# Conv products of all batches: the imaginary part accumulated in the first product's PSUM bank, copied out by ScalarE

## The chip, the cores and the metric

The kernel runs on one core of one Trainium2 chip. The metric is the device time of one execution in microseconds (us), taken as the median of several runs. Engines are named as in the profile: PE is TensorE (PEld its weight loads), DVE is VectorE, ACT is ScalarE, POOL is GpSimd, SP is SyncE, which issues nearly all DMAs. In the profile one fp32 matmul of the program is two passes on PE, so the profile counts 10004 PE instructions.

## The reference, cut to what matters

Two graph layers over 64 graphs of 256 nodes with 256 features, all in fp32. In the first layer:

```
h      = relu(bn1(conv1 @ x^T))                       # 1x1 convolution
x_conv = relu(bn2(conv2(h), 17 taps, along the nodes) + x)
A      = exp(-dist(x @ w_se)) * adj;  x_nmp = A @ relu(x @ w_msg)
gi     = [x_conv, x_nmp] @ w_ih^T;  gh = x @ w_hh^T   # GRU gates r, z, n
x      = layernorm(x + (1 - z) * n + z * x)
```

The second layer is a layernorm, an aggregation with `adj`, two 256x256 projections, a relu, a residual and a layernorm. The change concerns only the 17-tap convolution `conv2`.

## The kernel before, in words

**The convolution.** The graphs are handled in eight batches of eight. Each batch's sequences of 256 nodes are cut into overlapping pieces of 32, and the 17-tap convolution is done as a product of polynomials: DVE splits the data step by step into 15 complex residues and 2 real ones (`split`, `butterflies`), PE multiplies each residue by the filter's residue (a 256x256 matrix), and DVE merges them back (`merge`). A complex product takes three real ones: k1 is the filter's c times (re + im), k2 is (d - c) times re, k3 is (c + d) times im; the new real part is k1 - k3, the new imaginary part k1 + k2. The data lie in the SBUF tile `XF`, seen as slots `X` of 128 x 256; the sums re + im are in slots of their own. Each real product of one slot is four matmuls (two halves of the output features, two of the input features), of 128 moving columns each: eight passes on PE (L718).

**The groups.** Complex residues are multiplied in pairs, so that a group fills 512 columns of a PSUM bank. A batch has seven such groups (`products`, L721) and a last one of different shape (`last_products`, L759). For every batch but the first, the filter's residues come from DRAM: `load_w` (L706) loads three matrices (768 KB) for one residue into one of `W_DEEP` = 2 buffers in the tile `cs`. In the first batch (b = 0) all filters still lie in SBUF, in `w2all`.

**Two ways to end a group.** For b > 0, `products` uses three banks: p1, p2, p3. When all six products of the pair are done, ACT copies p1 to the slots of the sums (L735), DVE writes the real part as copy - p3 (L736) and the imaginary part as copy + p2 (L737). For b = 0, `products_added` (L740) uses two banks: the first product of both residues goes to p1, ACT copies p1 out (L748), the third goes to p3, and then the second product is accumulated onto p1, which now holds the imaginary part. ACT copies that to the data's slots (L755), and DVE does the one subtraction (L756).

**The rest of the work.** Beside the convolution, 32 pairs of graphs go through `pair`: messages (L1088), distances (L1125), aggregation (L1139), gates (L1191, a seven-product scheme for 2x2 block matrices; plain in L1177 for three pairs), normalisation, projection (L1366), second aggregation (L1380). The convolution of batch b + 1 is spread over the time in which the four pairs of batch b are worked on.

**What sets the order.** Nothing is issued in program order. All operations are recorded (`Program`, `Engine`), each with a key, which is a due time, and an estimated duration. `scheduled` (L320) then writes out one fixed order per engine: of the operations that could start, the one with the smallest key goes first; PSUM banks are handed out in the same pass, with at most three for the share "conv". PE operations that have been ready for 0.7 us are preferred (`READY`). The constants in L58 to L66 set the keys: `FIRST_GATES` and `PERIOD` when pairs are due, `CONV_FROM`, `CONV_OUT`, `CONV_TO` where a batch's convolution is spread, `LOAD_AHEAD` how much earlier than its place a load is keyed, `KEEP` the spacing of the copies of the finished convolution. On the chip each engine works through its list in order and waits where an input or a buffer is not there.

Of the kernel before, what the change touches and what calls it, by code (L numbers as in the profile page):

```python
# [32 lines left out]
NB = B // BG  # L33
# [21 lines left out]
OB = 7  # L55
HQ = 2 * M * C * (M + 1)
XC_SLOTS = BG + 2
FIRST_GATES, PERIOD, GATE_TIME = 115.5, 58.7, 14.1  # L58
AHEAD_FROM, AHEAD_TO, W_DEEP = -49.7, -53.1, 2
CONV1_FROM, CONV1_TO, CONV_FROM, CONV_OUT, CONV_TO = -29.4, 99.1, -10.5, -47.1, -26.3  # L60
PAIR_LEAD, FILTER_LEAD, LOAD_AHEAD = 50.5, 7.3, 20.3
SMALL_RUNS, TURN_FROM = 1.3, 2
KEEP = 13.3
LATE_LAG = 28.9
W_FROM, W_LAG = 2, 42.0
COORDS = 41.8  # L66
PLAIN, SUMS_FROM = (0, 1, B // 2 - 1), 2


# [349 lines left out]
def gnn_two_layers(  # L419
# [32 lines left out]
    def bank(name, share="rest"):  # L452
        return Space(name, [P, 512], "psum", share, share if share in ("conv", "gate") else None).view
# [127 lines left out]
    def sl(a, n, step=1):  # L581
        return X[:, a:a + n] if step == 1 else X[:, a:a + (n - 1) * step + 1:step]
# [123 lines left out]
    def load_w(b, first, n):  # L706
        if b == 0:
            return lambda m, c: W2[:, c, first + m, :]
        at = next(w2_at) * 3 * C * D
        t = cs[:, at:at + 3 * C * D].rearrange("p (m c o) -> p m c o", m=3, c=C)  # L710
        SP.dma_start(out=t[:, :n], in_=w2m[first:first + n].rearrange("f c p o -> p f c o"))
        return lambda m, c: t[:, m, c, :]

    def product(ps, slot, w, m, first=True):
        with prog.group():
            for o in range(C):
                for c in range(C):
                    PE.matmul(ps[:, o * P:(o + 1) * P], w(m, c)[:, o * P:(o + 1) * P], X[:, slot, c * P:(c + 1) * P],  # L718
                              start=first and o == 0 and c == 0, stop=(c == C - 1), skip_group_check=True)

    def products(b, first, sums):  # L721
        if b == 0:
            return products_added(first, sums)
        p1, p2, p3 = (bank(f"ps_k{i}", "conv") for i in (1, 2, 3))
        re, im, _ = LEAVES[first]
        for k in range(2):
            w = load_w(b, 3 * (first + k), 3)
            at = slice(k * D, (k + 1) * D)
            product(p1[:, at], sums + k, w, 0)
            product(p2[:, at], re + k, w, 1)  # L730
            product(p3[:, at], im + k, w, 2)

        def take():
            k1 = sl(sums, 2).rearrange("p s e -> p (s e)")
            A.copy(k1, p1)  # L735
            V.tensor_sub(sl(re, 2).rearrange("p s e -> p (s e)"), k1, p3)  # L736
            V.tensor_add(sl(im, 2).rearrange("p s e -> p (s e)"), k1, p2)  # L737
        return take

    def products_added(first, sums):  # L740
        p1, p3 = (bank(f"ps_k{i}", "conv") for i in (1, 3))
        re, im, _ = LEAVES[first]
        w = [load_w(0, 3 * (first + k), 3) for k in range(2)]
        at = [slice(k * D, (k + 1) * D) for k in range(2)]
        k1 = sl(sums, 2).rearrange("p s e -> p (s e)")
        for k in range(2):
            product(p1[:, at[k]], sums + k, w[k], 0, k == 0)
        A.copy(k1, p1)  # L748
        for k in range(2):
            product(p3[:, at[k]], im + k, w[k], 2)  # L750
        for k in range(2):
            product(p1[:, at[k]], re + k, w[k], 1, False)

        def take():
            A.copy(sl(im, 2).rearrange("p s e -> p (s e)"), p1)  # L755
            V.tensor_sub(sl(re, 2).rearrange("p s e -> p (s e)"), k1, p3)  # L756
        return take
# [102 lines left out]
    def conv(b):  # L860
# [8 lines left out]
        if b == 0:  # L869
            run(other)  # L870
        sv, s8, s4 = {}, {}, {}
        todo = [(lambda k=k: products(b, 2 * k, S + 2 * k), merges(0, k, S, sv, True)) for k in range(4)]
        todo += [(lambda k=k: products(b, 8 + 2 * k, S2 + 2 * k), merges(1, k, S2, s8, True)) for k in range(2)]
        todo += [(lambda: products(b, 12, S2 + 4), merges(2, 0, S2 + 4, s4, True)), (lambda: last_products(b), None)]
        vector = deque([other])
        share, spent = 61.0 / len(todo), 0.0
# [115 lines left out]
    def keep(steps, key):  # L992
        for q in range(BG // 2):
            prog.at(key + KEEP * q)
            next(steps, None)

    first = conv(0)
# [71 lines left out]
    def pair(p):  # L1069
# [37 lines left out]

        prog.at(due - COORDS, 0.3)
        V.transpose(turned.rearrange("p m e -> p (m e)"), st.rearrange("p m e -> p (m e)"))
# [447 lines left out]
```

## Time and profile before

| what | value |
|---|---|
| median of 3 runs | 1996.93 us (1996.78 to 1997.6) |
| the profiled execution | 1997.69 us, of which the span from the first to the last instruction is 1995.9 us |
| granted PE clock | 0.999 |
| busy: PE / DVE / ACT / POOL | 1983.0 / 1714.5 / 1014.0 / 282.2 us |
| DMA | 273.19 MB, mean 137 GB/s |

The profiled execution has 1.8 us around its span, and stands 0.8 us above the median. Busy times are unions: passes of matmuls overlap in PE's pipeline, so the sum of single durations is larger. A row of a group reads: line, engine, operation, output<-inputs, shape, count | busy us, mean ns of one | idle time of the engine just before, and what ended most of it. Of the eight batches of convolution products, the first runs from 76.8 to 137.3 us and uses `products_added`; the other seven run from 236.5 to 1754.2 us and use `products`.

### The profile page before, as it was taken

How to read it: one execution, taken by the hardware profiler on the slowest of the kernel's cores; microseconds unless marked ns; L12 is line 12 of the kernel's file. 1: busy time of each engine (PE TensorE's matmuls, PEld its weight loads, DVE VectorE, ACT ScalarE, POOL GpSimd, SP SyncE). 2: the span in 40 equal slices, each digit the busy share in tenths (PEclk: the TensorE clock that was granted, in tenths of full speed). 3: DMA queues.
4: the chain of work that ended last, by engine and by line, in shares of the span. 5: the costliest groups of instructions: out<-in, count | busy, mean ns of one | idle time of the engine just before them, and what ended most of it. 6: DMA issues, size and time to landing. Idle time of an engine off the chain costs nothing.

```text
span 1995.9 us, 28498 instructions
## 1 busy us (share of the span) xinstructions
PE 1983.0 (99%) x10004; PEld 1609.8 (81%) x10004; DVE 1714.5 (86%) x2664; ACT 1014.0 (51%) x2346; POOL 282.2 (14%) x522
## 2 busy tenths in 40 slices
PE   9999999999999999999999999999999999999998
PEld 6787789778987788878888788877898878887785
DVE  6786998999989999899988999899998999986655
ACT  7535443754446544565346544475444653466432
POOL 3100100111111111111011110111111111111001
PEclk9999999999999999999999999999999999999999
DMA  7844555345644455445554455444564325423221
GB/s 210 293 144 156 140 161 165 122 105 147 195 137 132 113 162 162 122 130 150 173 160 124 120 145 170 142 136 106 144 185 127 105 78 174 125 55 87 75 58 40
DMA packets 456685, 273.19 MB, mean 137 GB/s; under 512 B 253799, under 2 KB 441182, under 8 KB 456542
## 3 DMA queue, kind: packets, MB, share of 16 engines
q1 hardware_dynamic: 456000, 270.94, 46.9%
q8 instruction: 79, 1.29, 0.3%
q14 instruction: 64, 0.52, 0.1%
q10 hardware_dynamic: 542, 0.43, 0.1%
HBM read 194.10 MB, written 77.20 MB: 136 GB/s over the span
## 4 chain that ended last, share of the span: by engine, by line
PE 98%; DVE 1%; DMA 1%; issue 0%; ACT 0%; POOL 0%; SPq 0%; POOLq 0%; ACTq 0%; DVEq 0%
PE ps_a L1191 22%; PE ps_k L718 16%; PE ps_d L1191 11%; PE ps_hy L1366 11%; PE ps_msg L1088 6%; PE ps_nmp L1139 6%; PE ps_c L849 6%; PE ps_b L1191 6%; PE ps_agg L1380 5%; PE ps_g L1177 5%; PE ps_w L576 2%; PE ps_dist L1125 1%; PE ps_tT L559 0%; PE ps_xTc L828 0%; DMA w2m<-w2all 0%
## 5 line engine op out<-in xcount | busy, mean ns | idle before, releaser
L718 PEld LDWEIGHTS ps_k<-XF,cs 128*128 128x128 f32 x2632 | 311.4, 192 | 13.5 <-issue 8.1
L718 PE MATMUL ps_k<-XF,cs 128*128 128x128 f32 x2632 | 313.1, 275 | 0.0
L1366 PE MATMUL ps_hy<-wrr,wT 128*128 128x512 f32 x496 | 227.0, 594 | 0.0
L1191 PE MATMUL ps_a<-nmp,WB 128*128 128x256 f32 x696 | 207.0, 379 | 0.0
L1205 ACT ACTIVATE RG<-ps_a,bhh 128x512 f32<-128x512 f32 x116 | 79.5, 685 | 165.5 <-PE ps_a L1191 163.3
L1366 PEld LDWEIGHTS ps_hy<-wrr,wT 128*128 128x128 f32 x496 | 92.3, 190 | 87.9 <-issue 81.9
L1203 ACT COPY ZN<-ps_a 128x512 f32<-128x512 f32 x116 | 67.8, 584 | 183.9 <-PE ps_a L1191 183.5
L1191 PE MATMUL ps_a<-tx,WB 128*128 128x256 f32 x522 | 155.1, 380 | 1.9 <-ACT ZN L1203 1.9
L1191 PEld LDWEIGHTS ps_a<-nmp,WB 128*128 128x128 f32 x696 | 132.2, 190 | 18.0
L1088 PE MATMUL ps_msg<-wms,xT 128*128 128x260 f32 x512 | 133.3, 383 | 0.1
L690 DVE TENSOR_TENSOR XF<-XF 128x512 f32<-128x512 f32 (+3 forms) x128 | 126.6, 1007 | 5.5 <-ACT XF L771 4.0
L1368 DVE SCALAR_TENSOR_TENSOR HY<-ps_hy,q,hrow 128x512 f32<-128x512 f32 x124 | 92.8, 748 | 31.1 <-PE ps_hy L1366 28.4
L1139 PE MATMUL ps_nmp<-AT,msg 128*128 128x256 f32 x512 | 118.8, 379 | 0.5 <-DVE AT L1132 0.5
L1191 PEld LDWEIGHTS ps_a<-tx,WB 128*128 128x128 f32 x522 | 97.5, 190 | 26.0 <-issue 10.3
L1380 PE MATMUL ps_agg<-HY,adja 128*128 128x256 f32 x504 | 118.2, 379 | 0.0
L1380 PEld LDWEIGHTS ps_agg<-HY,adja 128*128 128x128 f32 x504 | 95.1, 190 | 28.3 <-issue 16.5
L1139 PEld LDWEIGHTS ps_nmp<-AT,msg 128*128 128x128 f32 x512 | 96.0, 190 | 13.4 <-DVE AT L1132 1.0
L1088 PEld LDWEIGHTS ps_msg<-wms,xT 128*128 128x128 f32 x512 | 94.9, 190 | 14.1 <-issue 1.4
L849 PE MATMUL ps_c<-xTc,w 128*128 128x512 f32 x232 | 106.1, 593 | 0.0
L1191 PE MATMUL ps_d<-nmp,WB 128*128 128x256 f32 x348 | 103.5, 379 | 0.0
L1191 PE MATMUL ps_a<-xc,WB 128*128 128x256 f32 x348 | 103.5, 379 | 0.0
L1191 PE MATMUL ps_a<-tc,WB 128*128 128x256 f32 x348 | 103.5, 379 | 0.0
(225 smaller groups left out, 4279.3 us busy)
## 6 DMA issues: line engine op xcount, KB each, us to landing
cs<-w2m SPq DMA_DIRECT2D x105, 768.0 KB
adjm<-in_adjT_dram SPq DMA_DIRECT2D x64, 256.0 KB
xT<-xt SPq DMA_DIRECT2D x32, 512.0 KB
adja<-in_adjT_dram SPq DMA_DIRECT2D x64, 256.0 KB
out_dram<-HY SPq DMA_DIRECT2D x63, 256.0 KB
hd<-xn SPq DMA_DIRECT2D x28, 544.0 KB
XF<-hd SPq DMA_DIRECT2D x28, 544.0 KB
xt<-xTc SPq DMA_DIRECT2D x29, 512.0 KB
```

What stands on the lines that cost most here:

```text
L690: (V.tensor_add if add else V.tensor_sub)(sl(o, n), sl(a, n), sl(b, n))
L718: PE.matmul(ps[:, o * P:(o + 1) * P], w(m, c)[:, o * P:(o + 1) * P], X[:, slot, c * P:(c + 1) * P], start=first and o == 0 and c == 0, sto ...
L849: PE.matmul(ps, w1[:, c, o * P:(o + 1) * P], xTc[:, c, :], start=(c == 0), stop=(c == C - 1), hold=[h[:, :, o]])
L1088: PE.matmul(ps[:, :D + 4], xT[:, c, g, m * P:(m + 1) * P], wms[:, c, :], start=(c == 0), stop=(c == C - 1 and not idle), hold=[msg[:, g, m]])
L1139: PE.matmul(ps[:, d * N:(d + 1) * N], msg[:, g, m, d * P:(d + 1) * P], AT[:, g, m, :], start=(m == 0), stop=(m == C - 1), hold=[nmp[:, :, g]])
L1177: PE.matmul(ps[:, h * N:(h + 1) * N], block[:, s, gate, :], right[s][2 * k + g], start=0 in ks and h == 0 and s == sources[0] and k == 0, ...
L1191: PE.matmul(ps[:, h * N:(h + 1) * N], block[:, s, gate, :], right[s][at], start=start and h == 0 and j == 0, stop=j == len(sources) - 1, s ...
L1203: A.copy(o, ps)
L1205: A.activation(o, ps, AF.Identity, bias=bhh[:, 2, f:f + 1])
L1366: PE.matmul(ps, wT[:, 2 * f + g, m * P:(m + 1) * P], wrr[:, f, :], start=(f == 0), stop=(f == C - 1), hold=[HY[:, g, m]], need=[q[:, 1, j: ...
L1368: stt(HY[:, g, m, :], ps, q[:, 1, j:j + 1], hrow)
L1380: PE.matmul(ps[:, n_ * D:(n_ + 1) * D], adja[:, g, m, n_ * P:(n_ + 1) * P], HY[:, g, m, :D], start=(m == 0), stop=(m == C - 1))
```

## The change

`products_added` takes the batch as an argument and is used for all eight batches (`ADDED_BELOW` = `NB` = 8). So for the 49 pair groups of b = 1 to 7, both filter loads are recorded ahead of the six products, the products stand in the order first, first, third, third, second, second (before: first, second, third of one residue, then of the other), the second ones go onto p1, and p2 is not used. The copy of p1 stands between the first and the second products. `last_products` is unchanged. Several constants of the order are other values; no constant of sizes or buffers is changed.

```diff
-FIRST_GATES, PERIOD, GATE_TIME = 115.5, 58.7, 14.1
-AHEAD_FROM, AHEAD_TO, W_DEEP = -49.7, -53.1, 2
-CONV1_FROM, CONV1_TO, CONV_FROM, CONV_OUT, CONV_TO = -29.4, 99.1, -10.5, -47.1, -26.3
-PAIR_LEAD, FILTER_LEAD, LOAD_AHEAD = 50.5, 7.3, 20.3
+FIRST_GATES, PERIOD, GATE_TIME = 116.6, 58.7, 14.1
+AHEAD_FROM, AHEAD_TO, W_DEEP = -44.8, -80.1, 2
+CONV1_FROM, CONV1_TO, CONV_FROM, CONV_OUT, CONV_TO = -29.5, 99.1, -10.5, -49.7, -27.2
+PAIR_LEAD, FILTER_LEAD, LOAD_AHEAD = 50.5, 8.6, 23.5
 SMALL_RUNS, TURN_FROM = 1.3, 2
-KEEP = 13.3
+KEEP = 14.5
 LATE_LAG = 28.9
-W_FROM, W_LAG = 2, 42.0
-COORDS = 41.8
+W_FROM, W_LAG = 2, 44.0
+COORDS = 41.3
+ADDED_BELOW = NB
...
     def products(b, first, sums):
-        if b == 0:
-            return products_added(first, sums)
+        if b < ADDED_BELOW:
+            return products_added(b, first, sums)
...
-    def products_added(first, sums):
+    def products_added(b, first, sums):
         p1, p3 = (bank(f"ps_k{i}", "conv") for i in (1, 3))
         re, im, _ = LEAVES[first]
-        w = [load_w(0, 3 * (first + k), 3) for k in range(2)]
+        w = [load_w(b, 3 * (first + k), 3) for k in range(2)]
```

## The prediction

> **What bounds the kernel now.** I read the page's busy times first, then the chain, then the busy time of each engine by stretches, because a share over the whole span hides where an engine is idle. Page, part 1 and part 4:
>
> ```profile
> PE 1983.0 (99%) x10004; PEld 1609.8 (81%) x10004; DVE 1714.5 (86%) x2664; ACT 1014.0 (51%) x2346; POOL 282.2 (14%) x522
> ...
> PE 98%; DVE 1%; DMA 1%; issue 0%; ACT 0%; POOL 0%; SPq 0%; POOLq 0%; ACTq 0%; DVEq 0%
> ```
>
> The chain that ended last is PE for 98%. Three stretches of the span (length, then busy time and instructions by engine in the order PE, PEld, DVE, ACT, POOL, then granted clock, DMA share, GB/s):
>
> ```profile
> 150.00:1572.00 1422.00, 1422.00 (x7218) 1161.24 (x7218) 1276.77 (x1927) 733.34 (x1713) 195.85 (x371) 1.00 0.50 144
> 1572.00:1760.00 188.00, 186.74 (x1011) 158.54 (x1010) 173.80 (x266) 87.65 (x224) 26.41 (x46) 1.00 0.41 116
> 1760.00:1995.90 235.90, 225.90 (x967) 177.07 (x965) 149.51 (x303) 110.39 (x233) 28.96 (x49) 0.99 0.22 62
> ```
>
> From 150 to 1572 us, where six of the seven changed batches lie, PE is not idle for a hundredth of a microsecond. A busy PE need not be a full one, so I also compared the starts of successive passes: passes of 128 columns follow each other by 112 ns, those of 256 by 216 ns, through all this stretch, apart from some 0.7 us around each of the 32 distance blocks (L1125), which the change leaves alone. PE there is at its pace. The other idle time of PE is 1.26 us in the second stretch and 10.0 us in the third; of the latter 6.8 us lie after the last matmul (it ends at 1989.07 of 1995.90) and 2.04 us before the last aggregation (L1419). So a faster DVE has nothing to shorten in most of the span.
>
> **What is removed and added.** The rows of the two engines, each group with its shape:
>
> ```profile
> L736 DVE TENSOR_TENSOR XF<-XF,ps_k 128x512 f32<-128x512 f32 x49 | 33.4, 682 | 16.8 <-PE ps_k L718 16.6
> L737 DVE TENSOR_TENSOR XF<-XF,ps_k 128x512 f32<-128x512 f32 x49 | 33.3, 679 | 0.0
> ...
> L735 ACT COPY XF<-ps_k 128x512 f32<-128x512 f32 x49 | 28.7, 585 | 72.3 <-PE ps_k L718 72.2
> L748 ACT COPY XF<-ps_k 128x512 f32<-128x512 f32 x7 | 4.1, 587 | 12.2 <-PE ps_k L718 9.8 <-issue 2.4
> ```
>
> DVE loses the 49 adds of L737: 49 x 0.679 = 33.3 us, to 1681 us (84%). ACT gains 49 copies: 49 x 0.587 = 28.8 us, to 1043 us (52%). Neither engine is on the chain in the changed stretch, so both count as 0 in the sum; what hides them is PE's own 1422 us. PE has the same 10004 passes in the built kernel, and accumulating is nothing new to it (two of every four matmuls of a product add onto the bank already): 0. POOL's and SP's instructions keep their numbers (SP 1156 DMAs).
>
> **The new wait on PE.** The second products may not start before ACT has copied p1. The wait stands in PE's in-order list, so gates, projections and aggregations queued behind it wait too, and through them ACT and DVE. The first batch has this form already. One of its copies, and the ACT and DVE work after it:
>
> ```profile
> 106.75 0.59 ACT L748 COPY XF<-ps_k 128x512 f32<-128x512 f32 x1 [3.88 <-PE ps_k L718]
> 107.65 0.59 ACT L755 COPY XF<-ps_k 128x512 f32<-128x512 f32 x1 [0.31 <-PE ps_k L718]
> 107.72 0.69 DVE L756 TENSOR_TENSOR XF<-XF,ps_k 128x512 f32<-128x512 f32 x1 [3.92 <-PE ps_k L718]
> ```
>
> The last pass of p1 ends at 106.72, the copy runs from 106.75 to 107.34, the first accumulating pass starts at 107.45. Between them stood only the eight passes of the third product, 8 x 0.112 = 0.90 us. In the two groups with this least cover one pass of PE came late by 0.046 and by 0.101 us; in the five with more (from about 1.6 us) none did, so ACT's path costs about 0.9 us. Now the order of the built kernel: I counted PE's work between p1's last pass and the first accumulating one, at the intervals above, for the 49 new groups. Two have 1.54 us, five 1.77, the other 42 at least 2.6: PE does other work in between. Bounds for the wait: 0, or 49 x 0.101 = 4.9 us if all stood as the tightest. Not one new group has as little cover as those two, so I take the lower end, with 0.1 us for each of the two at 1.54: 0.2 us. ACT is in order too: a copy behind one of its longest operations (L913, 1.26 us a piece) needs 0.9 + 1.26 = 2.2 us, within the cover of 42 groups; the seven others could lose 0.4 to 0.6 us if they met one.
>
> [...]
>
> **The filter loads.** Before, a residue's buffer was free after its three products; now both are in use until the second products at the end, so the next group's loads start later. From the two orders I counted PE's work from the last use of a buffer to the first use of its next content: before, the least is 6.56 us and one load of 112 has under 7.0; after, the least is 6.49 and 13 have under 7.0. What a load needs is bounded by the trace. SP's issue and the product that uses it (1.95 and 1.05 are runs of 16 and 8 passes):
>
> ```profile
> 482.75 0.36 SPq L711 DMA_DIRECT2D cs<-w2m  x1
> ...
> 485.61 1.95 PE L718 MATMUL ps_k<-XF,cs 128*128 128x128 f32 x16
> 487.58 0.36 SPq L711 DMA_DIRECT2D cs<-w2m  x1
> ...
> 489.11 1.05 PE L718 MATMUL ps_k<-XF,cs 128*128 128x128 f32 x8
> ```
>
> The load issued at 482.75 is first used at 489.11, 6.36 us later, the shortest such distance, and PE did not wait. So 6.36 us is enough; 768 KB at 293 GB/s, the busiest slice of the page, would be 2.7 us, a lower end. SP mostly issues 0.03 us after the buffer is free, but its queue can be held: one buffer was free at 467.45 and its load issued at 471.62, 4.17 us later, behind other DMAs; the order had left 12.6 us of cover there. With a prompt issue even the upper end fits (6.36 + 0.03 under 6.49): 0 us. If SP were held by 4.17 us at one tight load, it would be 2.7 + 4.2 - 6.5 = 0.4 us late, or 4.1 us by the upper end. I take 0.3 us in all. What waits behind a late load is PE's whole list.
>
> [...] The row alone leaves 0.1 us of room.
>
> **Who else waits.** DVE's merges of a pair now need ACT's second copy. In the first batch that cost DVE 0.3 us in seven groups; for 49 it is 2 us of DVE idle, beside PE's work. The constants move other operations; counted the same way, the remaining hand-overs from ACT and DVE to PE have covers like before. Two stalls stay where they were: at 1599.13 and 1823.33 us PE waits for a copy of the gates (L1203). In the first the copy stands behind four operations of L1314 that wait for a DMA, and the same four stand in front of it in the new order. Of the last 71 entries of PE's list none moves, so the tail is the same.
>
> **Sum.** The profiled execution of 1997.69 us gets 0 - 0 + 0 + 0.2 + 0.3 = +0.5; the median of 1996.93 becomes about 1997.4, rounded to 1997.3 since both terms are upper guesses. 0.2% (4.0 us) is about what a measurement of this kernel can tell from no change.
>
> **Rivals.** First, DVE bounds the kernel (86% busy), and 33.3 us come off: 1963.6. Against it stands PE's idle time of 0 in 1422 us; all idle time of the span is 12.9 us. Chance 0.01. Second, the looser DVE and the new constants close the stalls inside the span: by the starts of passes 1.42 (at 1599) + 0.84 (at 1823) + 0.61 (at 1884, for DVE's L1132) = 2.9 us, which gives 1994.1. For it: DVE has 33 us more room; against it: the first two wait for ACT. Still within 0.2%. Chance 0.10; another 0.02 for more than that. Third, slower: filter loads come late. Place: the first product of a group, at the 13 loads with under 7 us. Price: at 0.5 us each 6.5 us, which gives 2003.4; it decides from 4.0 / 13 = 0.31 us each, that is if a load takes about 7.2 us from the free buffer. For it: the 4.17 us that SP was once held, and 13 tight places instead of one; against it: 6.36 us was enough. Chance 0.09. Fourth, the copies queue on ACT so that PE waits in all 49 groups by 0.1 us: 4.9 us, 2001.8. Against it: cover of 2.6 us in 42 groups. Chance 0.03. That the change is not made is no rival: the order has 49 more copies on ACT and 49 fewer operations on DVE. The forecast keeps 0.75.
>
> **How the numbers follow.** Faster by over 0.2% is the first rival and the extra 0.02: 0.03. Slower is the third and fourth: 0.12. The rest, 0.85, is within. The range goes from the second rival, 1994.1, to 3.4 us above the forecast, 2000.7: one tight load held at the dearer price, or the seven groups of little cover losing 0.5 us each.
>
> **What would show it.** In the profile after: PE again without idle time from 150 to 1572 us; L737's row gone from DVE and 56 copies each of L748 and L755 on ACT (lines one further down); L718 without a wait for ACT's copy or for `cs`. The prediction is wrong if PE has idle time at L718 released by ACT's copy of `XF` (the fourth rival) or by a DMA `cs<-w2m` (the third), or if the span falls below 1992.

## The result and the profile after

The changed kernel takes 2006.75 us (median of 5 runs, 2004.59 to 2008.05) against 1997.13 us (5 runs, 1996.78 to 1998.03): a ratio of 1.0047, 95% interval 1.0036 to 1.0059, so 9.6 us slower. The profiled execution took 2006.35 us with a span of 2004.5 us, 8.6 us more than before. Page, parts 1 and 4:

```profile
PE 1987.6 (99%) x10004; PEld 1614.2 (81%) x10004; DVE 1686.8 (84%) x2615; ACT 1039.4 (52%) x2395; POOL 276.0 (14%) x522
...
PE 97%; DVE 2%; DMA 0%; ACT 0%; issue 0%; SPq 0%; POOLq 0%; POOL 0%; DVEq 0%; ACTq 0%
```

The same three stretches by engine (the last reaches to the end of the longer span):

```profile
150.00:1572.00 1422.00, 1417.86 (x7189) 1158.34 (x7188) 1247.65 (x1878) 751.18 (x1748) 194.47 (x368) 1.00 0.50 143
1572.00:1760.00 188.00, 185.89 (x981) 156.93 (x980) 170.66 (x258) 93.55 (x234) 25.95 (x46) 0.99 0.41 116
1760.00:2004.50 244.50, 235.14 (x1021) 185.58 (x1019) 153.51 (x311) 111.74 (x238) 27.61 (x49) 0.99 0.24 64
```

DVE lost its 49 operations and 27.7 us, ACT gained 49 and 25.4 us. But PE, never idle between 150 and 1572 us before, now is for 4.1 us, and the chain has 2% of DVE in place of 1%. The group that carries most of that idle time is not one of the changed lines:

```profile
L1192 PE MATMUL ps_a<-xc,WB 128*128 128x256 f32 x348 | 103.8, 380 | 3.3 <-ACT xc L1147 3.3
```

It is the gates of one pair of graphs, waiting for `xc`, the relu of a finished convolution. The timeline of the kernel after shows the place (start, duration, engine, line, operation, count; in brackets the idle time before and its releaser):

```profile
387.95 0.69 DVE L908 SCALAR_TENSOR_TENSOR XF<-XF 128x512 f32<-128x512 f32 x1
390.28 1.28 DVE L908 SCALAR_TENSOR_TENSOR XF<-XF 128x512 f32<-128x512 f32 x2
...
394.69 1.22 DVE L1146 TENSOR_TENSOR xc<-xc,xT 128x1024 f32<-128x1024 f32 x1
395.94 1.06 ACT L1147 ACTIVATE xc<-xc 128x1024 f32<-128x1024 f32 x1 [0.30 <-DVE xc L1146]
...
397.05 0.92 PE L1192 MATMUL ps_a<-xc,WB 128*128 128x256 f32 x2 [3.30 <-ACT xc L1147]
```

DVE's last merge steps (L908) run until 391.6, the residual (L1146) and the relu (L1147) follow, and PE stands for 3.30 us at pair 4, the first that needs batch 1's convolution. The kernel before had the same residual 20 us earlier:

```profile
369.61 1.28 DVE L907 SCALAR_TENSOR_TENSOR XF<-XF 128x512 f32<-128x512 f32 x2
...
374.09 1.22 DVE L1145 TENSOR_TENSOR xc<-xc,xT 128x1024 f32<-128x1024 f32 x1
```

The stall costs more than its idle time. The stretches around it in the kernel after (length, busy time by engine in the order of above, granted clock, DMA share, GB/s):

```profile
393.50:397.05 3.55, 0.25 (x3) 0.00 (x1) 3.55 (x7) 3.25 (x6) 2.35 (x3) 1.00 0.00 0
397.05:401.20 4.15, 4.15 (x11) 3.37 (x12) 3.98 (x8) 4.15 (x9) 0.79 (x1) 0.59 0.26 86
```

For 4 us after it the granted clock is 0.59, and passes of 256 columns follow each other by 0.43 us in place of 0.216: another 1.9 us.

To place the rest, I took for every pass the time since the start of the pass before it, less the median of that interval for its shape in the kernel before. PE's work at that pace is 1954.4 to 1954.7 us in every kernel below, so the time beyond it is what differs. In us, with three runs of the next section beside:

| stretch | before | after | after, second profile | constants alone | batch 1 alone |
|---|---|---|---|---|---|
| 360 to 470 | 1.5 | 6.8 | 6.8 | 1.6 | 8.0 |
| 1060 to 1170 | 1.5 | 1.5 | 1.5 | 4.9 | 1.5 |
| 1540 to 1650 | 3.0 | 5.6 | 5.6 | 2.5 | 2.5 |
| 1880 to the last pass | 4.1 | 6.5 | 6.1 | 5.0 | 5.0 |
| all else | 24.6 | 23.5 | 25.5 | 24.9 | 26.0 |
| sum | 34.7 | 43.9 | 45.5 | 38.9 | 43.0 |
| last pass to the end | 6.8 | 6.1 | 6.0 | 6.8 | 6.8 |

Of the 8.6 us, 5.3 lie at pair 4 (360 to 470), 2.6 at the stall of 1599 us in the profile before, which is now at 1605, and 2.4 at the end; 1.1 and 0.7 come back. Of the 2.4, 0.6 is no loss: a distance block (L1125) that stood at 1879 us before stands at 1887 after, and so has moved from "all else" into the last stretch. (The batch 1 alone and second-profile columns lose another 1.4 and 0.9 us elsewhere, in small pieces.)

### The profile page after: what moved, and what is told of

It is laid out like the page before. It is cut to its first block, busy times and chain, and to the rows that moved or that the text cites. A ratio compares the mean times of both kernels' runs of the same rounds, so it can differ in the third digit from the quotient of the medians.

```text
span 2004.5 us, 28491 instructions
## 1 busy us (share of the span) xinstructions
PE 1987.6 (99%) x10004; PEld 1614.2 (81%) x10004; DVE 1686.8 (84%) x2615; ACT 1039.4 (52%) x2395; POOL 276.0 (14%) x522
## 4 chain that ended last, share of the span: by engine, by line
PE 97%; DVE 2%; DMA 0%; ACT 0%; issue 0%; SPq 0%; POOLq 0%; POOL 0%; DVEq 0%; ACTq 0%
PE ps_a L1192 22%; PE ps_k L719 17%; PE ps_d L1192 11%; PE ps_hy L1367 11%; PE ps_b L1192 6%; PE ps_nmp L1140 6%; PE ps_msg L1089 5%; PE ps_agg L1381 5%; PE ps_c L850 5%; PE ps_g L1178 4%; PE ps_w L577 2%; PE ps_dist L1126 1%; PE ps_tT L560 0%; PE ps_xTc L829 0%; DMA cs<-w2m 0%; PE ps_hy L1358 0%
## 5 line engine op out<-in xcount | busy, mean ns | idle before, releaser
L719 PEld LDWEIGHTS ps_k<-XF,cs 128*128 128x128 f32 x2632 | 325.5, 192 | 29.7 <-issue 20.3
L719 PE MATMUL ps_k<-XF,cs 128*128 128x128 f32 x2632 | 327.1, 275 | 0.0
L1204 ACT COPY ZN<-ps_a 128x512 f32<-128x512 f32 x116 | 67.6, 582 | 136.4 <-PE ps_a L1192 136.1
L1192 PEld LDWEIGHTS ps_a<-tx,WB 128*128 128x128 f32 x522 | 95.6, 190 | 23.5 <-issue 8.2
```

The source lines that it names most:

```text
L1192: PE.matmul(ps[:, h * N:(h + 1) * N], block[:, s, gate, :], right[s][at], start=start and h == 0 and j == 0, stop=j == len(sources) - 1, s ...
L1204: A.copy(o, ps)
```

## The experiments

Theory 1: the groups hold the filter buffers longer, so batch 1's products end later and its output is late for pair 4 (further down, 1a: because the shared bank's copy needs both filters; 1b: merely because both loads stand ahead and the second products last). Theory 2: it is the changed constants, not the products. Theory 3: PE waits for ACT's copies. Three sets of comparisons, with medians of before of 1997.17, 1997.13 and 1997.32 us.

**Does it repeat?** The changed kernel, profiled again.

> The changed kernel, unaltered, profiled a second time, on another chip than its first profile perhaps. If the late output of batch 1's convolution belongs to the order, TensorE again waits 3 us or more near 397 us for the gates' input xc, followed by passes of half pace, and the span is 2003 to 2007 us. If it was an accident of one execution, there is no idle time there and the lost time stands elsewhere.

2007.94 us, span 2006.2 us. The timeline of this second profile:

```profile
398.73 0.70 PE L1192 MATMUL ps_a<-xc,WB 128*128 128x256 f32 x2 [3.30 <-ACT xc L1147]
```

The same wait, with slow passes after it (granted clock 0.61 from 398.7 to 403 us), and the same 5.6 us around 1605: both belong to the order.

**The constants.** First the new constants with the products as before:

```diff
-ADDED_BELOW = NB
+ADDED_BELOW = 1
```

> The new constants with the products as before (three banks for batches 1 to 7). Theory 1 (held buffers): 1996 to 2000 us, batch 1's products end near 348 us, no idle time of PE near 397. Theory 2 (constants): 2003 us or more, with PE idle near 397 by about 3 us.

2001.92 us (1999.57 to 2003.7), ratio 1.0021 (1.0012 to 1.0031): 4.8 us, between what the two theories gave. Batch 1's products end at 349.3 and its relu at 378.4, 13.5 us ahead of use; no wait near 397. In the profiled execution the loss is a single wait elsewhere, 3.07 us at 1135, where a copy of the gates (L1204) stands on ACT behind L1337, which waits for POOL. None of the other kernels with these constants shows that one. Then the reverse, the change with the constants of before:

```diff
-FIRST_GATES, PERIOD, GATE_TIME = 116.6, 58.7, 14.1
+FIRST_GATES, PERIOD, GATE_TIME = 115.5, 58.7, 14.1
... (likewise all the other changed constants but ADDED_BELOW)
```

> The change with all constants of before. Theory 1 (held buffers: both filter buffers are in use until the end of a group, so batch 1's products end late, at 356.6 us instead of 348.2, and pair 4 waits for its convolution): as slow as after or slower, 2003 to 2030 us, batch 1's products end at 356 us or later, and PE is idle near 397 us by 3 us or more. Theory 2 (the moved constants let the end of batch 1's convolution slip): 1996 to 1999 us, no idle time of PE near 397.

2025.32 us (2024.85 to 2026.08), ratio 1.0140 (1.0125 to 1.0155): 28 us. The timeline has the wait twice, at the gates that need batch 1 and batch 7:

```profile
400.61 1.22 PE L1192 MATMUL ps_a<-xc,WB 128*128 128x256 f32 x2 [7.62 <-ACT xc L1147]
...
1825.88 1.22 PE L1192 MATMUL ps_a<-xc,WB 128*128 128x256 f32 x2 [9.31 <-ACT xc L1147]
```

So the two parts do not add, and theory 2 is no more than a part: the new constants cost 4.8 us by themselves and save the change 19 us. They leave of these waits the 3.3 us at pair 4.

**The place.** Batch 1 left as it was, then batch 1 alone changed:

```diff
-        if b < ADDED_BELOW:
+        if b != 1:
```

> As after, but batch 1 takes three banks as before (batches 0 and 2 to 7 are changed). Theory 1 (held buffers, which hurt where a batch has no slack, in batch 1): the 3.3 us of PE idle time near 397 us and the 1.9 us of slow passes behind it are gone, 2000 to 2003 us. Theory 2 (constants): the idle time stays and the time is within 1 us of after, about 2006.5. Theory 3 (PE's new wait for ACT's copies, a little in each of 49 groups): one seventh of the loss goes, 2005.

```diff
-        if b < ADDED_BELOW:
+        if b < 2:
```

> The changed kernel with its constants, but only batch 1 (and, as before, batch 0) accumulates; batches 2 to 7 use three banks and VectorE's second addition. Theory 1a: a group of batch 1 has the least time until its output is wanted, so the wait of some 3 us near 397 us is there in full though only 7 of the 49 groups are changed, and the time is 2004 to 2007 us. A price that is spread over all 49 groups (theory 3) would leave 7/49 of the 4.8 us that the change adds on top of its constants: 2002.6 us, and no idle time near 397 us.

Without batch 1: 2005.25 us (2003.18 to 2007.07), ratio 1.0039 (1.0024 to 1.0054), above theory 1's 2000 to 2003. The wait near 397 is gone, and one of its kind stands at the first batch that is changed, batch 2 (timeline):

```profile
635.89 0.70 PE L1192 MATMUL ps_a<-xc,WB 128*128 128x256 f32 x2 [2.78 <-ACT xc L1147]
```

With batch 1 alone: 2006.11 us (2005.73 to 2007.49), ratio 1.0044 (1.0031 to 1.0058), and the wait is there in full:

```profile
398.38 1.22 PE L1192 MATMUL ps_a<-xc,WB 128*128 128x256 f32 x2 [3.29 <-ACT xc L1147]
```

Seven groups cost about as much as 49, and 6.5 us of it lie at pair 4 by the table, so theory 3's price for each group falls. The stretch around 1605 loses 2.5 us here, as with the constants alone; its extra 2.6 us need the later batches.

**What holds the buffers.** A late group of batch 1 in the kernel after, the timeline's rows of the products and loads:

```profile
325.83 1.05 PE L719 MATMUL ps_k<-XF,cs 128*128 128x128 f32 x8
326.92 2.99 SPq L712 DMA_DIRECT2D cs<-w2m  x2
328.45 1.05 PE L719 MATMUL ps_k<-XF,cs 128*128 128x128 f32 x8
...
334.53 1.95 PE L719 MATMUL ps_k<-XF,cs 128*128 128x128 f32 x16
338.03 1.95 PE L719 MATMUL ps_k<-XF,cs 128*128 128x128 f32 x16
339.14 0.58 ACT L749 COPY XF<-ps_k 128x512 f32<-128x512 f32 x1
340.69 1.05 PE L719 MATMUL ps_k<-XF,cs 128*128 128x128 f32 x8
341.78 0.37 SPq L712 DMA_DIRECT2D cs<-w2m  x1
```

The second products of the group before (325.83 and 328.45) free the buffers, two loads go out, PE comes to them at 334.53. The first residue's first and third product are done at 336.5, but its second must wait for ACT's copy of the bank (339.14), and that for the second residue's first product and so for its filter. Only after 340.69 is the first buffer free, at 341.78. From first to last use, the 14 loads of batch 1 issued from 244.0 us on keep their buffers for 7.13 us in the mean; before, the 14 issued from 239.4 on kept them for 3.76. From issue to first use they have 8.28 us after and 11.19 before. So one turn of a buffer takes 15.4 us in place of 14.95: the order makes up for most of the longer use by giving the loads less time, down to 6.31 us in the tightest case, which still was enough. Batch 1's products end 8.5 us later (356.6 against 348.2). Of this, 4.5 us are the later start, since the first group already holds both buffers until its second products, and 3.2 us the seven turns of each buffer, each 0.46 us longer. Three kernels take a part of this away. First, each load in three pieces of 256 KB, in the order of use:

```diff
-        SP.dma_start(out=t[:, :n], in_=w2m[first:first + n].rearrange("f c p o -> p f c o"))
+        for m in (0, 2, 1)[:n] if n == 3 else range(n):
+            SP.dma_start(out=t[:, m:m + 1], in_=w2m[first + m:first + m + 1].rearrange("f c p o -> p f c o"))
```

> As after, but each filter load of 768 KB is three loads of 256 KB, in the order in which the products use them, so that each third of a buffer comes free after its own product. Theory 1 (held buffers): batch 1's products end near 348 us again, PE is not idle near 397, 1997 to 2001 us. Theory 2 (constants): 2005 us or more, idle near 397 as after. Theory 3 (PE's wait for ACT's copies): 2005 us or more.

2002.76 us (2001.19 to 2004.22), ratio 1.0026 (1.0015 to 1.0037), not quite down to the 2001 that theory 1 gave at most. The products end at 346.4, and no wait is near 397: the time is back near the level of the constants alone. The stall of 1605 us is still there in its profile, with 2.26 us. Second, everything as after, but the second products in a bank of their own:

```diff
-            product(p1[:, at[k]], re + k, w[k], 1, False)
+            product(p2[:, at[k]], re + k, w[k], 1, b > 0)
...
+            if b > 0:
+                V.tensor_add(sl(im, 2).rearrange("p s e -> p (s e)"), k1, p2)
```

> The changed kernel with its constants, its two loads ahead of the six products and its order of products (first, first, third, third, second, second), but for batches 1 to 7 the second products go to a bank of their own and VectorE adds them, as before the change; TensorE waits for no copy inside a group. Theory 1a (what delays batch 1 is that the bank's copy needs both filters before the first filter's buffer can be given back): batch 1's products end near 349 us of the span as with the constants alone (349.3), there is no idle time of TensorE near 397 us, and the median lies at the level of the constants alone, 2000 to 2003 us. Theory 1b (it is the two loads recorded ahead and the second products standing last, whatever bank they go to): batch 1's products still end at 354 us or later, TensorE still waits some 3 us near 397 us, 2004 to 2007 us. Theory 3 (TensorE's waits for ScalarE's copies) expects the level of the constants alone too, but no change of batch 1's end.

The products end at 349.9 and a load of batch 1 is in use for 4.91 us; no wait near 397, as theory 1a says and 1b does not. But the time is above what theory 1a gave: 2006.0 us (4 runs, 2003.85 to 2011.18), ratio 1.0046 (1.0030 to 1.0061). The profiled execution is the fastest of the four; in it PE waits 2.07 us at 1609 us for an operation of DVE (L1137, on `AT`), a wait that no other of these kernels has at this place. Where the other executions lost 2 to 7 us more, it can't show. So this run shows what delays batch 1, not what the delay is worth. Third, accumulation kept, with a bank for each residue:

```diff
+        ps = [bank("ps_k1", "conv"), bank("ps_k2", "conv")]
+        p3 = bank("ps_k3", "conv")
+        for k in range(2):
+            w = load_w(b, 3 * (first + k), 3)
+            product(ps[k][:, :D], sums + k, w, 0)
+            A.copy(X[:, sums + k, :], ps[k][:, :D])
+            product(p3[:, k * D:(k + 1) * D], im + k, w, 2)
+            product(ps[k][:, :D], re + k, w, 1, False)
```

> The changed kernel with its constants and with accumulation, but for batches 1 to 7 each residue of a pair has a bank of its own, of which it uses 256 columns: first product, copy of 256 columns, third product, second product accumulated, then the other residue; one filter load ahead of each residue's products, as before the change. ScalarE makes four copies of 256 columns for a group in place of two of 512; VectorE has the one subtraction. Theory 1a: a residue's buffer is free again without the other residue's filter, so batch 1's products end near 349 us, no idle time of TensorE near 397 us, 2000 to 2003 us. Theory 3: TensorE's wait for a copy comes twice in a group with 0.9 us of cover from the third product alone, so the loss grows: 2008 us or more, with idle time at the products' line released by ScalarE's copy.

2001.79 us (2000.88 to 2004.8), ratio 1.0023 (1.0014 to 1.0032), the level of the constants alone. Batch 1's products end at 348.3. PE from 360 to 401 us (order of above), and PE's row for all products of batches 1 to 7:

```profile
360.00:401.20 41.20, 41.20 (x174) 31.41 (x173) 37.96 (x59) 30.74 (x56) 3.13 (x6) 1.00 0.42 135
...
L719 PE MATMUL ps_k<-XF,cs 128*128 128x128 f32 x2632 | 318.4, 275 | 0.0
```

41.20 us are busy of 41.20 where the kernel after stood still. All groups accumulate here, each with two copies that PE has to wait for, and PE is never idle ahead of a product. So theory 3 falls again, and what delays batch 1 is the copy of a bank that both residues share, not accumulating. (This kernel also has the products of a group in another order and its loads apart; the one before it changed neither, and batch 1 was on time there too.)

**With other constants.** The split loads, and the bank for each residue, with the constants of before:

> The changed kernel (shared bank) with each load of 768 KB cut into three of 256 KB in the order of use, and the constants of the kernel before. Theory 1a with the buffers' turn as the price: cutting the loads shortens the wait from a free buffer to the first product, so most of the 28 us that the change cost with these constants is gone: 1996 to 2002 us. If the loads' latency is not the price, the time stays above 2010 us, with the convolution's output late for the gates near 400 and near 1826 us.

2000.15 us (1999.14 to 2002.5), ratio 1.0015 (1.0006 to 1.0025): of the 28 us that the change costs with these constants, cutting the loads takes 25 away.

> The same two banks for a pair, with the constants of the kernel before. If the constants alone cost what they did when they were tried without the change (4.8 us) and the banks take the change's own part away, 1996 to 2000 us: the accumulation as such costs nothing. If the accumulation asks for other constants, as the changed kernel with the constants of before did (2025 us), 2005 us or more, with the convolution's output late for a pair's gates at one or more batches.

A miss: 2004.54 us (2003.34 to 2006.04), ratio 1.0034 (1.0020 to 1.0048). No gates wait for `xc`; PE waits 7.8 us in all for copies of the gates (L1224). In the four longest waits (947, 1186, 1424 and 1605 us, 6.1 us together) the copy stands on ACT behind four operations that wait for the DMA `x<-wd`. That is the stall of 1599 us in the profile before, now in four places. Last, constants searched anew for the bank for each residue and, as a measure, for the kernel before:

> A bank for each residue of the pair, accumulation in all batches, and constants of the order searched anew for this form of the product. If what the accumulation costs is only that the order has to be made anew around it, this kernel reaches the kernel before or passes it by a few us: 1993 to 1998 us. If the accumulation itself costs TensorE time (its waits for ScalarE's copies, 0.9 us of cover in a group), no constants bring it below 2000 us.

> The kernel before with other constants of the order alone (PERIOD 58.41, AHEAD_FROM -35.05, CONV1_FROM -32.85, CONV1_TO 91.99, CONV_OUT -49.74, CONV_TO -28.84, LATE_LAG 25.62, W_LAG 41.3), no change of the products: the measure for the kernel with a bank for each residue and constants searched in the same way. If constants alone move this kernel by several us either way, as the changed kernel's constants did (+4.8 us), 1993 to 1996 us here, and the gain of the other one is not due to accumulation. If the kernel before already stands at what its order can give, 1997 us or more.

1999.01 us (1997.74 to 2001.05), ratio 1.0008 (0.9999 to 1.0017), and 1998.42 us (1996.96 to 1999.87), ratio 1.0005 (0.9996 to 1.0014). The first is 1 us above what was expected and below the 2000 that would have spoken against accumulating. Neither can be told from the kernel before. So with the buffers freed in time and an order that fits, accumulating in all batches costs nothing that these runs can tell, and it gains nothing.

## Why the prediction was wrong

**What bounds the kernel: right.** PE has no room (99% busy in both pages), DVE's 27.7 us less (33.3 forecast for the removed operations) shortened nothing, and ACT's 25.4 us more never held PE at the products.

**The new wait on PE, 0.2 us, and the filter loads, 0.3 us: right at their place.** PE's row for the products, from the page after:

```profile
L719 PE MATMUL ps_k<-XF,cs 128*128 128x128 f32 x2632 | 327.1, 275 | 0.0
```

PE was never idle ahead of a product, neither for a copy of L749 nor for a load. The one wait for a load in the view of the tile `ps_k` is of PEld, the weight loads beside PE:

```profile
DMA cs<-w2m: 0.2, 1
```

(0.2 us, once). So none of the signs by which the prediction wanted to be found wrong came. But the first sign of its being right failed: PE has 4.1 us of idle time from 150 to 1572 us, 3.3 of it at a line that the change doesn't touch.

**The step that failed** is in "Who else waits": "the remaining hand-overs from ACT and DVE to PE have covers like before". I had counted cover between one operation and the next, and sized a late buffer only by whether PE waits at that load. The order had avoided those waits by placing the groups later. The price was paid at the end of the chain: products, merge on DVE, relu, gates. In the kernel before that chain takes 29.1 us (348.2 to 377.3), and PE reaches the gates 41.6 us after the products. After, it takes 40.4 us (356.6 to 397.0), and PE is there after 36.6 us. Of the chain's extra 11 us, about 10 are DVE's: its L908 steps take 373.3 to 391.6 us instead of 8.4 us, since other work of its list, 377 to 388 us, stands between them. The longer chain comes with the later end: where batch 1's products end between 346 and 350 us (constants alone, split loads, own bank, bank for each residue) it takes 26.5 to 31.0 us. An engine that got 28 us lighter over the span was full just where it mattered: from 360 to 393.5 us it is 95% busy, as it was before (94%), so it had no room to catch up.

The order itself had forecast much of this. `scheduled` keeps an estimated start and end of each operation, computed from the code and not measured: by these the last operation ends at 1983.7 us in the kernel before and at 1990.4 in the kernel after, and from 387 to 395 us PE's plan has 5.1 us of idle time, just ahead of pair 4's gates, where the plan before has none. The prediction counted covers in this order and left its times unread.

The third rival named the right resource, the buffers freed later, and, by luck, a time of the right size (2003.4 us), but not how: its price was 0.5 us at each of 13 loads, where no load was late. The table gives 5.3 us at one pair of graphs.

**"Two stalls stay where they were": half right.** The second kept its 0.68 us (at 1831 us now). The first stayed in place but grew. Timeline of ACT in the kernel after:

```profile
1602.80 0.42 ACT L1315 ACTIVATE HY<-x 128x256 f32<-128x256 f32 x1 [3.57 <-DMA x<-wd]
...
1604.42 0.56 ACT L1204 COPY ZN<-ps_a 128x512 f32<-128x512 f32 x1
```

The same four operations stand ahead of the copy, as predicted, but the DMA holds them for 3.57 us (2.72 before), PE stands for 2.11 us (1.26 before), and then the granted clock is 0.58 from 1605.05 to 1609 us, where it was 1.00 after the wait before: 2.6 us in all. Why it comes only with the later batches changed was not tried by itself. **"The tail is the same"** failed by the clock alone (0.53 at the last aggregation in place of 1.00): the order there is unchanged.

**The constants** were counted at nothing ("move other operations"). They cost 4.8 us alone and are worth 19 us to the change; with a scheduler's constants in the diff, the chance of 0.85 for no change was far too high.

## What to carry to other kernels

Where an order is planned, a resource that is held longer need not show as a wait for that resource: here the plan moved the work back, and the time was lost at the last consumer of the whole stage. So follow the changed stage to where its output is needed, and compare the length of that chain with the other engine's work up to there, batch by batch, the first one before all, and read the plan's own times. Accumulating onto a bank that had to be copied in between tied together the two residues that shared it: a load of batch 1 kept its buffer for 7.13 us in place of 3.76, and batch 1's products ended at 356.6 us; with a bank for each residue they ended at 348.3.

## What was not expected of the hardware

In these runs idle times of PE of 2.0 to 3.3 us cost up to twice their length, but not always. After 3.30 us of idle time, at 397 us in the kernel after, the granted clock was 0.59 for 4 us, and the stretch lost 5.3 us by the table. After 3.29 us with batch 1 alone it was 0.50 from 398.4 to 402.6 us, and the stretch lost 6.5. After 3.07 us, at 1135 us with the constants alone, the stretch lost 3.4: the second pair of passes of 256 columns took 0.59 us there, and 1.06 behind the wait of 3.30 us. After the last wait of 2.04 us, before the last aggregation, the clock differs from kernel to kernel: 1.00 before, 0.53 after. Stretches of before, then of after:

```profile
1986.90:1989.00 2.10, 2.10 (x8) 1.32 (x8) 1.26 (x4) 1.44 (x3) 0.00 (x0) 1.00 0.00 0
```

```profile
1994.80:1998.40 3.60, 3.59 (x8) 2.44 (x8) 1.98 (x6) 1.45 (x3) 0.00 (x0) 0.53 0.22 73
```

The eight passes take 3.6 us in place of 2.1, which is most of what is lost at the end. The second profile of the kernel after has it too (0.56), the kernel with batch 1 alone does not (1.00).

Half pace also came after 2.11 us of idle time (at 1605 us, clock 0.58). So by these runs the length of an idle time alone does not tell whether slow passes follow: they did after 2.04 and 2.11 us, and did not after 3.07. What decides it, no trace here shows.
